# Identity matmuls ahead of the slot layer's transposes, sums and projections

## The chip, the cores and the metric

The kernel runs as one program on one core of a Trainium2 chip. The metric is the device time of one execution in microseconds (us). The kernel before takes 2276.86 us, the median of three runs (2275.09 to 2281.09 us).

The engines are named as in the profile: PE is the matrix engine, PEld its weight loads, DVE the vector engine, ACT the scalar engine, POOL the general engine, and SP the engine that issues most of the DMAs. Each engine works through its own instructions in order; between engines, instructions wait for semaphores.

## The reference

A residual network of eight sublayers works on `x` of 4 batches, 1024 tokens and 128 features, all in float32; after each sublayer comes a layer norm over the features of the sum of the input and the sublayer's output. The sublayers are a two-layer minGRU, the slot layer, a sparse attention, a two-expert feed-forward, a linear attention, a routed feed-forward with eight experts, a state-space scan and a second routed feed-forward. The change touches the slot layer and the step behind it:

```python
h = gelu(concat([x, slot_mean]) @ w1 + b1)                 # 64 hidden features
logits = (h @ w2 + b2) / (abs(tau) + 0.1)                  # 64 slots
alpha = softmax of the top 8 logits, scattered to the 64 slots
si = einsum('bts,btd->bsd', alpha, x) / (alpha.sum(1) + 1e-8)
S_new = GRU cell(si, slot_init)                            # gates r, z and n
q, k, v = S_new @ wq + bq, S_new @ wk + bk, S_new @ wv + bv
y = layernorm(S_new + softmax(q k^T * DQ**-0.5) v) * ln_g + ln_b
out = einsum('bts,bsd->btd', alpha, y @ wvp + bvp) @ wo + bo
x = layernorm(x + out)
```

The sparse attention that follows projects queries and keys of `x`, measures each query against 35 sampled keys (maximum less mean), and attends only for the 35 best queries of each head.

## The kernel before, in words

Tokens are held twice: `xN[b]` has 128 tokens on the partitions and eight chunks of 128 features, and `xT[b]` has the 128 features on the partitions and 1024 tokens. `to_features` makes the second from the first with PE transposes (the helper `tr`, L133, multiplies by the identity `self.ident`) into a PSUM bank called `pt`, four chunks to a bank, and an ACT copy (L143). All other matmuls go through the helper `mm` (L129), so the profile shows most of them under that one line and tells them apart by their tiles.

`front` runs the first sublayers. Generators for the batches are taken in turn by `weave`, which only sets the order in which instructions are written. The final order on each engine is set by a scheduler that plays the program on a timeline of its own, and that keeps to the data's order and to the PSUM banks. For the slot layer the eight banks are divided into the pools `u` (two banks, used by the update and by the first choice of queries), `p0` (three banks, batches 0 and 2) and `p1` (three banks, batches 1 and 3). These pool names exist in `self.psq` in this stage only; the minGRU ahead of it and the attention behind it use other names. In the linear attention (`l2_attn`) the order on PE is written out by hand.

The slot layer's steps, with the tile names under which the profile shows them:

- `l0_route`, once for each batch: `ph` (two halves of 512 tokens) and a Gelu on ACT into `hT`, which has two buffers; the logits `pl` (eight matmuls of 64 columns) and their copy `lg` on ACT (L302); on DVE the eight largest of each token (L306, L307) and the masked exponentials `ex`; the weights `al` on POOL (L321); eight transposes of `al` and an ACT copy into `alT`; the slot sums `psi`, eight matmuls that accumulate; on DVE the quotient `si` (L342), one transpose of it, and the ACT copy `siT`.
- `l0_update`, once, for all batches together: gates `pg` and `pn`, with DVE and ACT between them; `sn`, the new slots; the projections `pq` (twice, queries and keys) and `pv`; the scores `psc`; a softmax on DVE and ACT into `sat`; its transposes `pat`; the sum `py` (for each batch one matmul by the identity and one by the attention); a norm on DVE; the transposes `pyt`; the projections `psv` and `pso`, and the DVE copy into `svo`.
- `l0_read`, for batches 0 and 1 and then, beside the first choice of queries, for 2 and 3: for each half of the tokens `po` (four matmuls), a DVE sum into `slot_r` (L479), `norm_parts` on DVE and ACT (which writes `xN` at L176), and `to_features`. Each half is stored to DRAM (`xd`) by SP.
- `l1_measure` follows for each batch: `px` (sums of the sampled tokens by a one-hot matrix, 35 columns), `pk`, `pq` (512 columns), `pm` (280 columns) and a DVE maximum of it into `mall` (L569). `l1_choose` transposes `mall`, copies it to `mT` (L583), takes five rounds of top-8 on DVE (L588 to L591) and casts the indices (L595 to L600); SP takes them through DRAM, and POOL gathers the chosen rows (`xgs`, L645).

Of the kernel before, what the change touches and what calls it, by code (L numbers as in the profile page):

```python
# [20 lines left out]
P = 128  # L21
# [39 lines left out]
class Net:  # L61
# [66 lines left out]
    def mm(self, out, lhsT, rhs, start=True, stop=True):  # L128
        return self.nc.tensor.matmul(out=out, lhsT=lhsT, rhs=rhs, start=start, stop=stop)  # L129

    def tr(self, out, in_):
        n = in_.shape[0]
        self.nc.tensor.transpose(out, in_, self.ident[0:n, 0:n])  # L133

    def to_features(self, src, b, c0, g, ps=None):

        for c1 in range(0, g, 4):
            n = min(4, g - c1)
            pt = ps([P, n, P], "pt")
            for c in range(n):  # L140
                self.tr(pt[:, c, :], src[:, c1 + c, :])
            o = (c0 + c1) * P
            self.nc.scalar.copy(  # L143
                self.xT[b][:, o : o + n * P], pt.rearrange("p a b -> p (a b)")
            )
# [141 lines left out]
    def l0_route(self, b, ps, W, wp):  # L287

        nc, alT = self.nc, W["alT"][b]
        hT = wp.tile([DH + 1, T], F32, name="hT")  # L290
        nc.gpsimd.memset(hT[DH : DH + 1, :], 1.0)
        for h in range(2):
            s = slice(h * 512, h * 512 + 512)
            ph = ps([DH, 512], "ph")
            self.mm(ph, W["w1"][:, 0, :], self.xT[b][:, s])
            nc.scalar.activation(hT[0:DH, s], ph, AF.Gelu, bias=W["hb"])
        yield
        pl = ps([P, NC, NS], "pl")
        for k in range(NC):
            self.mm(pl[:, k, :], hT[:, k * P : (k + 1) * P], W["w2"])  # L300
        lg = wp.tile([P, NC, NS], F32, name="lg")
        nc.scalar.copy(lg, pl)  # L302
        top = wp.tile([P, NC, 8], F32, name="top")
        rep = wp.tile([P, NC, NS], F32, name="rep")
        for k in range(NC):
            nc.vector.max(top[:, k, :], lg[:, k, :])  # L306
            nc.vector.match_replace(rep[:, k, :], top[:, k, :], lg[:, k, :], NEG)  # L307

        ex = wp.tile([P, NC, NS], F32, name="ex")
        nc.vector.tensor_tensor(  # L310
            ex, pl, top[:, :, 0:1].to_broadcast([P, NC, NS]), ALU.subtract
        )
        nc.vector.tensor_tensor(rep, rep, pl, ALU.not_equal)
        nc.scalar.activation(ex, ex, AF.Exp, scale=W["rt"])
        yield
        nc.vector.tensor_mul(ex, ex, rep)
        es = wp.tile([P, NC], F32, name="es")
        nc.vector.reduce_sum(es, ex, AX.X)
        nc.vector.reciprocal(es, es)
        al = wp.tile([P, NC, NS], F32, name="al")  # L320
        nc.gpsimd.tensor_mul(al, ex, es[:, :, None].to_broadcast([P, NC, NS]))  # L321
        yield
        dn = wp.tile([NS, 2], F32, name="dn2")
        for h in range(2):
            pt = ps([NS, 4, P], "pt")
            for k in range(4):
                self.tr(pt[:, k, :], al[:, 4 * h + k, :])
            nc.scalar.activation(
                alT[0:NS, h * 512 : h * 512 + 512],
                pt.rearrange("p a b -> p (a b)"),  # L330
                AF.Copy,
                accum_out=dn[:, h : h + 1],
            )
        psi = ps([NS, D], "psi")
        for k in range(NC):
            self.mm(psi, al[:, k, :], self.xN[b][:, k, :], k == 0, k == NC - 1)
        yield
        rd = wp.tile([NS, 1], F32, name="rd")
        nc.vector.tensor_scalar(rd, dn[:, 0:1], dn[:, 1:2], 1e-8, ALU.add, ALU.add)
        nc.vector.reciprocal(rd, rd)  # L340
        si = wp.tile([NS, D], F32, name="si")
        nc.vector.tensor_scalar_mul(si, psi, rd)  # L342
        pt = ps([P, NS], "pt")
        self.tr(pt, si)
        nc.scalar.copy(W["siT"][:, b, :], pt)
        yield

    def l0_update(self, ps, W, pool):
# [20 lines left out]
            rz.append(g)  # L369
        yield  # L370
        pn = ps([P, 2, BS], "pn")
        self.mm(pn[:, 1], wg[:, 1, 2 * D :], s2)
        self.mm(pn[:, 0], wg[:, 0, 2 * D :], si)
        nn = wp.tile([P, BS], F32, name="nn")
# [13 lines left out]
        qk = []  # L388
        for w, nm in ((wq, "s_bq"), (wk, "s_bk")):
            pq = ps([DQ, BS], "pq")  # L390
            self.mm(pq, w, snf)
            t = wp.tile([DQ, N, NS], F32, name=f"t_{nm}")
            nc.vector.tensor_scalar_add(
                t.rearrange("p b s -> p (b s)"), pq, self.col(nm, DQ)
            )
            qk.append(t)
# [4 lines left out]
        nc.vector.tensor_add(v, pv, rows[:, 0:1, :].to_broadcast([NS, N, D]))  # L401
        yield
        psc = ps([NS, N, NS], "psc")
        for b in range(N):
            self.mm(psc[:, b, :], qk[0][:, b, :], qk[1][:, b, :])
        mx = wp.tile([NS, N], F32, name="smx")
# [8 lines left out]
        nc.vector.reciprocal(mx, mx)  # L415
        nc.vector.tensor_mul(at, at, mx[:, :, None].to_broadcast([NS, N, NS]))
        pat = ps([NS, N, NS], "pat")
        for b in range(N):
            self.tr(pat[:, b, :], at[:, b, :])
        att = wp.tile([NS, N, NS], F32, name="satT")  # L420
        nc.vector.tensor_copy(att, pat)
        yield
        py = ps([NS, N, D], "py")
        for b in range(N):
            self.mm(py[:, b, :], sn[:, b, :], self.ident, start=True, stop=False)
            self.mm(py[:, b, :], att[:, b, :], v[:, b, :], start=False, stop=True)
# [17 lines left out]
        nc.vector.tensor_add(y, y, rows[:, 2:3, :].to_broadcast([NS, N, D]))  # L444
        yield
        pyt = ps([P, N, NS], "pyt")
        for b in range(N):
            self.tr(pyt[:, b, :], y[:, b, :])
        yT = wp.tile([P, BS], F32, name="syT")
        nc.vector.tensor_copy(yT, pyt.rearrange("p b s -> p (b s)"))  # L450
        yield
        psv = ps([P, BS], "psv")
        self.mm(psv, wvp, yT)
        svT = wp.tile([P, N, NS], F32, name="svT")
        nc.vector.tensor_scalar_add(
# [2 lines left out]
        yield  # L458

        pso = ps([NS, N, D], "pso")  # L460
        for b in range(N):
            self.mm(pso[:, b, :], svT[:, b, :], wo)
        nc.vector.tensor_copy(W["svo"][0:NS], pso)
# [1747 lines left out]
```

## Time and profile before

| What | Value |
|---|---|
| Median of three runs | 2276.86 us (2275.09, 2276.86, 2281.09) |
| The profiled execution: its time, its span | 2279.28 us, 2277.5 us |
| Busy of the span: PE, PEld, DVE, ACT, POOL | 1977.3, 1385.7, 1348.0, 1198.7, 1024.1 us |
| Matmul passes on PE | 17788 |
| Mean clock of PE | 0.935 of full speed |
| Route (first `ph` to last `psi`) | 79.84 to 118.9 us |
| Update (first `pg` with `siT` to `svo`) | 120.24 to 148.5 us |
| Read and measure, batches 0 and 1 | 148.58 to 192.05 us |
| Read and measure, batches 2 and 3 | 191.49 to 242.8 us |

The profile comes from one execution, and its times are positions in its span. An engine's idle time ahead of an instruction is put down to what ended it ("<-"). In a timeline, a row stands for instructions of one form in succession: start, length from the first start to the last end, engine, line, operation, output and inputs, shape, count. The clock of PE is the share that the throttle granted, from 0.5 to 1.00 in this trace.

### The profile page before, as it was taken

How to read it: one execution, taken by the hardware profiler on the slowest of the kernel's cores; microseconds unless marked ns; L12 is line 12 of the kernel's file. 1: busy time of each engine (PE TensorE's matmuls, PEld its weight loads, DVE VectorE, ACT ScalarE, POOL GpSimd, SP SyncE). 2: the span in 40 equal slices, each digit the busy share in tenths (PEclk: the TensorE clock that was granted, in tenths of full speed). 3: DMA queues.
4: the chain of work that ended last, by engine and by line, in shares of the span. 5: the costliest groups of instructions: out<-in, count | busy, mean ns of one | idle time of the engine just before them, and what ended most of it. 6: DMA issues, size and time to landing. Idle time of an engine off the chain costs nothing.

```text
span 2277.5 us, 46329 instructions
## 1 busy us (share of the span) xinstructions
PE 1977.3 (87%) x17788; PEld 1385.7 (61%) x17788; DVE 1348.0 (59%) x3668; ACT 1198.7 (53%) x2610; POOL 1024.1 (45%) x812
## 2 busy tenths in 40 slices
PE   6667979979999999999979876679899999998998
PEld 3455655544477777787867664346565656565666
DVE  7647743433355555655565556696877688777521
ACT  6523433332244444444555455577768786767443
POOL 5100320000123235234243318998889989879400
PEclk9667989979999999999999987799999999999999
DMA  3000110005000010031222047456776677776421
GB/s 107 0 19 19 34 35 10 10 25 159 1 3 3 3 36 21 16 89 44 80 77 83 25 131 231 129 175 207 209 212 174 183 188 190 194 187 177 110 61 51
DMA packets 138555, 211.09 MB, mean 93 GB/s; under 512 B 18596, under 2 KB 75933, under 8 KB 137950
## 3 DMA queue, kind: packets, MB, share of 16 engines
q1 hardware_dynamic: 126190, 173.87, 25.4%
q0 software_dynamic: 12144, 34.26, 7.2%
q8 instruction: 140, 2.29, 0.4%
q14 instruction: 81, 0.66, 0.1%
HBM read 160.29 MB, written 23.16 MB: 81 GB/s over the span
## 4 chain that ended last, share of the span: by engine, by line
PE 43%; DVE 13%; ACT 11%; issue 3%; POOL 1%; DMA 1%; SPq 0%; ACTq 0%; DVEq 0%; POOLq 0%
PE py L129 8%; PE ph L129 7%; PE po L1127 5%; PE pqk L129 5%; PE pa_m L129 4%; DVE db L1855 4%; PE kp_mo L129 2%; PE pys L129 2%; PE pv L129 2%; PE pr L1197 2%; ACT da L1854 2%; ACT hh L1981 1%; PE pt L133 1%; PE kp_mo L133 1%; ACT xN L176 1%
## 5 line engine op out<-in xcount | busy, mean ns | idle before, releaser
L1060 POOL TENSOR_TENSOR qt<-r_q,sb_c_turn 128x256 f32<-128x256 f32 (+1 forms) x256 | 164.4, 663 | 451.5 <-ACT r_q L1052 445.9
L1866 POOL TENSOR_TENSOR hc<-db,cn 128x1024 f32<-128x1024 f32 x128 | 317.9, 2522 | 55.7 <-PE pys L129 28.2
L129 PEld LDWEIGHTS py<-wh,hh 128*128 128x128 f32 x2048 | 252.1, 193 | 81.6 <-issue 46.2
L1850 POOL TENSOR_TENSOR db<-ud,bn 128x1024 f32<-128x1024 f32 x112 | 290.7, 2679 | 12.4 <-issue 9.9
L129 PE MATMUL py<-wh,hh 128*128 128x128 f32 x2048 | 259.8, 278 | 14.2 <-ACT hh L1981 7.5
L129 PE MATMUL ph<-xT,wh 128*128 128x512 f32 x512 | 253.1, 610 | 21.3 <-DVE h_acc L1997 6.2
L1981 ACT ACTIVATE hh<-ph,sb_cols 128x512 f32<-128x512 f32 x256 | 170.6, 681 | 119.9 <-PE ph L129 93.2
L1118 DVE TENSOR_TENSOR a<-pa_m,sb_c_near 128x256 f32<-128x256 f32 x256 | 96.5, 419 | 205.0 <-PE pa_m L129 205.0
L1075 ACT ACTIVATE kN<-kp_mo,sb_c_trig 128x128 f32<-128x128 f32 x448 | 130.2, 372 | 131.5 <-PE kp_mo L133 121.6
L1854 ACT ACTIVATE da<-dl,aneg 128x512 f32<-128x512 f32 x224 | 153.4, 689 | 76.1 <-DVE db L1855 75.0
L129 PE MATMUL pys<-hc,sb_c_ident 128*128 128x512 f32 x324 | 159.6, 623 | 21.6 <-POOL hc L1866 19.6
L1855 DVE TENSOR_TENSOR_SCAN db<-da,carry,db 128x512 f32<-128x512 f32 x128 | 157.0, 1265 | 13.3 <-ACT da L1854 9.4
L1855 DVE TENSOR_TENSOR_SCAN db<-da,db 128x512 f32<-128x512 f32 x128 | 149.2, 1204 | 10.4 <-POOL db L1850 6.0
L129 PEld LDWEIGHTS ph<-xT,wh 128*128 128x128 f32 x512 | 88.4, 193 | 101.7 <-issue 52.4
L1997 DVE SCALAR_TENSOR_TENSOR h_acc<-py,gt,h_acc 128x128 f32<-128x128 f32 x256 | 71.9, 342 | 129.5 <-PE py L129 129.5
L129 PE MATMUL pqk<-xT,wE 128*128 128x256 f32 x512 | 138.3, 394 | 8.2 <-ACT coT L1194 4.2
L129 PEld LDWEIGHTS pys<-hc,sb_c_ident 128*128 128x128 f32 x324 | 61.1, 200 | 85.6 <-issue 59.0
L731 POOL DMA_INDIRECT orows<-o,ix x20 | 18.9, 946 | 187.5 <-DVE o L729 160.9
L129 PEld LDWEIGHTS pqk<-xT,wE 128*128 128x128 f32 x512 | 89.6, 195 | 22.2 <-DVE cv L1037 8.1
L1194 ACT COPY coT<-pt 128x512 f32<-128x512 f32 x64 | 37.6, 587 | 117.1 <-PE pt L133 117.1
L133 PE MATMUL pt<-sb_c_ident,xN 128*128 128x128 f32 x224 | 52.7, 342 | 48.7 <-ACT xN L176 29.0
L129 PE MATMUL po<-ht,wD 128*128 128x512 f32 x192 | 93.7, 595 | 0.0
(453 smaller groups left out, 4328.5 us busy)
## 6 DMA issues: line engine op xcount, KB each, us to landing
wx<-in_wF SPq DMA_DIRECT2D x92, 384.0 KB, 3.5
bn<-rows SPq DMA_DIRECT2D x128, 256.0 KB, 4.7
cn<-rows SPq DMA_DIRECT2D x128, 256.0 KB, 4.2
wh<-in_wH SPq DMA_DIRECT2D x64, 512.0 KB, 3.8
hc<-hc POOLq DMA_DIRECT2D x47, 512.0 KB, 6.6
xrows<-zero SPq DMA_DIRECT2D x4, 1472.0 KB, 13.1
xg<-xrows SPq DMA_DIRECT2D x20, 256.0 KB, 3.2
yrows<-ys SPq DMA_DIRECT2D x20, 256.0 KB, 3.2
```

The lines of the kernel that those rows point to most:

```text
L129: return self.nc.tensor.matmul(out=out, lhsT=lhsT, rhs=rhs, start=start, stop=stop)
L133: self.nc.tensor.transpose(out, in_, self.ident[0:n, 0:n])
L1060: nc.gpsimd.tensor_mul(u["qt"][:, m, a:], u["q"][:, a:], c2["turn"][:, m, o + a : o + 2 * P])
L1075: self.nc.scalar.activation(u["kN"][:, c, m, :], pk[:, c, :], AF.Copy, scale=trig[:, k, m : m + 1])
L1118: nc.vector.tensor_mul(u["a"][:, i, :, :], pa[i], self.c2["near"][:, None, :].to_broadcast([P, 2, P]),)
L1127: self.nc.tensor.matmul(out=u["po"][self.HALF[j], i, c, :], lhsT=lhsT, rhs=rhs, start=key not in u["begun"], stop=True, skip_group_check=True,
L1850: nc.gpsimd.tensor_mul(db, ud, bc[0])
L1854: nc.scalar.activation(da, dl[:, ec, :], AF.Exp, scale=aneg[:, j : j + 1])
L1855: nc.vector.tensor_tensor_scan(db[:, ec, :], da, db[:, ec, :], carry[:, ec, n : n + 1] if h else 0.0, ALU.mult, ALU.add,)
L1866: nc.gpsimd.tensor_mul(hc, db, bc[1])
L1981: nc.scalar.activation(ht, ph, AF.Relu, bias=self.col("h_b1", i=e * NK + k))
L1997: nc.vector.scalar_tensor_tensor(acc[:, c, :], py[:, c, :], gt[:, c, e : e + 1], acc[:, c, :], ALU.mult, ALU.add,)
```

## The change

A helper `warm` writes `n` matmuls (eight unless said otherwise) of the identity by the identity into a tile that the code is about to fill. It does so only where the pool `p0` exists, that is in this stage. It is called ahead of the transposes in `to_features`, of the logits `pl` and the slot sums `psi` in the route, and of `pn`, `pq` (4 each), `psc`, `pat`, `py`, `pyt`, `psv` and `pso` in the update. The real matmuls start their banks anew, so the results of the helper are overwritten.

```diff
+    def warm(self, out, n=8):
+
+        if "p0" in self.psq:
+            p, o = out.shape[0], out[:, 0] if len(out.shape) == 3 else out
+            for k in range(n):
+                self.mm(o, self.ident[:, 0:p], self.ident[:, 0 : o.shape[1]])
...
             pt = ps([P, n, P], "pt")
+            self.warm(pt)
             for c in range(n):
                 self.tr(pt[:, c, :], src[:, c1 + c, :])
...
         pl = ps([P, NC, NS], "pl")
+        self.warm(pl)
...
         psi = ps([NS, D], "psi")
+        self.warm(psi)
...
         pn = ps([P, 2, BS], "pn")
+        self.warm(pn[:, 0, 0:P], 8)
...
             pq = ps([DQ, BS], "pq")
+            self.warm(pq[:, 0:P], 4)
...
         psc = ps([NS, N, NS], "psc")
+        self.warm(psc, 8)
...
         pat = ps([NS, N, NS], "pat")
+        self.warm(pat, 8)
...
         py = ps([NS, N, D], "py")
+        self.warm(py, 8)
...
         pyt = ps([P, N, NS], "pyt")
+        self.warm(pyt, 8)
...
         psv = ps([P, BS], "psv")
+        self.warm(psv[:, 0:P], 8)
...
         pso = ps([NS, N, D], "pso")
+        self.warm(pso, 8)
```

In the changed program's order on PE, the helper's matmuls stand as follows. Those of `pl` are directly ahead of each batch's logits. Those of `psi` are behind the eight transposes of `al` of the same batch, directly ahead of the slot sums. In the update they are directly ahead of their real matmuls, but for `py` (its helper matmuls and its first real one stand ahead of the transposes `pat`) and `psv` (ahead of the transposes `pyt`). In the read of batches 0 and 1, 16 stand between the first and the second halves' `po` and 16 more ahead of and among the first transposes; in that of batches 2 and 3, 5 stand between the two first `po`, 11 behind the second, 12 behind the second halves' `po`, and 4 among the transposes. The helper adds 192 matmuls in all.

## The prediction

> **What bounds the kernel now.** I read the page's slices first, then windows of 25 and 2 us over the slot layer, the waits in it, and the timelines of PE, DVE, ACT and POOL from 80 to 330 us. The chain that ended last is followed back only to 613.99 us, so it says nothing of the slot layer (75 to 250 us); from there on it is one unbroken chain, so what the slot layer gains or loses should reach the end about one to one.
>
> ```profile
> PE   6667979979999999999979876679899999998998
> PEclk9667989979999999999999987799999999999999
> ```
> One digit is 57 us. The clock is below full in the first slices, where PE is also the least busy.
>
> ```profile
> 100.00:125.00 25.00, 16.50 (x108) 13.34 (x108) 17.61 (x75) 8.47 (x25) 4.17 (x4) 0.82 0.00 1
> 125.00:150.00 25.00, 14.78 (x60) 9.18 (x61) 10.44 (x30) 2.00 (x3) 0.00 (x0) 0.59 0.00 0
> 150.00:175.00 25.00, 21.19 (x87) 17.76 (x86) 9.95 (x50) 11.43 (x29) 0.00 (x0) 0.52 0.15 43
> 175.00:200.00 25.00, 18.77 (x98) 11.07 (x96) 19.05 (x59) 5.85 (x11) 0.00 (x0) 0.95 0.00 1
> 200.00:225.00 25.00, 18.12 (x73) 15.48 (x74) 23.59 (x60) 10.81 (x26) 4.67 (x2) 0.50 0.14 42
> ```
> Columns: length, then busy time of PE, PEld, DVE, ACT and POOL, then the clock. From 125 to 175 us PE runs at half clock and is the busiest engine; from 200 us DVE is, with 23.6 of 25 us. A faster PE is thus worth much in the first stretch and little in the second.
>
> In the 2 us windows the clock steps at 95.4 (down), 109.0 (up), 126.1 (down), 129.5 (up), 132.9 (down), 173.9 (up), 197.8 (down), 225.1 (up): all apart by multiples of 3.41 us. It falls after a stretch that was mostly idle (122.64 to 125.59) or held only the 64-column logits (pl, 91.9 to 95.4). It does not rise from 163.6 to 170.4, when PE runs transposes and 35-column px without a break, and rises once pq of 512 columns fills a stretch.
>
> ```profile
> PE pt L133 <- ACT xN L176: 16.9, 4, 6.6
> PE pt L133 <- POOL al L321: 9.8, 2, 9.7
> ```
> Of PE's waits, these two are the long ones.
>
> ```profile
> 86.89 2.00 PE L129 MATMUL pl<-sb_w_slot,hT 65*128 65x64 f32 x16
> 109.81 1.06 PE L133 MATMUL pt<-sb_c_ident,al 128*64 128x128 f32 x8
> 110.81 1.96 PE L129 MATMUL psi<-xN,al 128*64 128x128 f32 x16
> 125.59 1.49 PE L129 MATMUL pq<-sn,sb_w_slota 128*32 128x256 f32 x4 [2.95 <-DVE sn L385]
> 127.01 1.97 PE L129 MATMUL pv<-sb_w_slota,sn 128*64 128x128 f32 x8
> 132.43 0.38 PE L133 MATMUL pat<-sb_c_ident,sat 64*64 64x64 f32 x4 [2.60 <-DVE sat L416]
> 142.86 0.66 PE L133 MATMUL pyt<-sb_c_ident,sy 64*128 64x64 f32 x4 [5.16 <-DVE sy L444]
> 169.69 3.76 PE L129 MATMUL pq<-xT,sb_w_sp 128*128 128x512 f32 x4
> ```
> A matmul of f32 is two passes here (8 psi matmuls are x16). A pass of 128 columns takes 0.122 us at full clock (psi) and 0.246 at half (pv); so one warm of eight 128-column matmuls takes 1.96 or 3.9 us, and one of 64 columns into 128 rows 1.9 us (pl).
>
> **The change, part by part.** It adds 192 matmuls (384 passes) on PE in banks that the real work then overwrites, removes none, and issues no DMA. Each warm waits for its bank alone, and everything later on PE waits behind it. Where it stands in PE's order decides. L2's own order on PE is unchanged; later orders differ only by swaps of a few places (L3 among them), for which I take 0 and 3 us either way.
>
> Route, warms of pl (four times 16 passes). Before, PE ran from 79.84 to 95.4 without a wait, so nothing hides them. The first logits end at about 91.7 instead of 88.85; ACT does two Gelus first (they wait for hT, which the logits free), and lg goes from 90.14 to 93.05. DVE starts 2.9 us later. The new DVE order finishes batch 0 before going on, so al of batch 0 comes at 106.7 instead of 105.1 on PE.
>
> Route, warms of psi. In the new order they stand behind the transposes of al, which wait for POOL: the 9.7 us wait is not filled. Each batch now takes PE 1.0 (pt) + 1.96 (warm) + 1.96 (psi) = 4.9 us, where batches came every 3.1 us (109.81, 112.92, 116.01). From 106.7 the first takes 1.9 + 3.9 + 2.0 us while the clock is still half, the others 4.9 each: the last psi ends at 129.2 instead of 118.9, and pg, 1.3 us later, starts at 130.5 instead of 120.24: +10.2 us. If the clock stays full before al, +8.5; if the longer pl stretch loses it at 95.4, its last 64 passes run at 0.21 us (px x10 in 2.19 us at half clock, also small columns) instead of 0.12, al of the later batches comes late, and it is +13. I take +11, nearer to the upper end since the trace does lose the clock in pl.
>
> Update (times relative to pg). The warm of pn has no wait to hide in: pn came 0.1 us after pg. It delays nn by 1.3 us (DVE's gates end only at 122.66). The warm of pq (2 x 4) lies in the 2.95 us wait for sn. pq, pv and psc drop from 4.24 to 2.4 us at full clock, less 0.85 for psc's warm: now +0.5. pat's and py's warms (0.85 + 1.96) and the first py (0.25) stand ahead of pat and exceed the 2.60 us wait, since py's bank is free only after DVE's sat: +1.2. py's eight pairs go from 5.0 to 2.3 us: -1.35. pyt's and psv's warms (3.9) lie in the 5.16 us wait; pyt and psv get 0.9 us shorter: -2.2. pso's warm (1.96) has a 0.58 us wait: +1.4; pso is 1.0 shorter: -1.8; the first po 0.95 shorter, so DVE's slot_r starts 2.85 us earlier than it would.
>
> Read of batches 0 and 1. 32 warm matmuls, 7.8 us at full clock. The first 16 run while DVE and ACT normalise; po of the second halves, which stood behind the first transposes, now stand before them. Second halves reach ACT's xN 0.8 to 1.5 us earlier; px, pt, pk and pq run in 11 instead of 16 us. The first pm comes at 170.4 instead of 177.29: -6.9 from pg on, update included. The other end: the stretch of pt and px loses the clock as it failed to raise it in the trace, pk comes 2.5 us later and pq runs at half clock again: -1.9. I take -4.
>
> The Trainium skill ("TensorE: Matmul & The Clock Gate", Part 4) states that transposes do not count as PE being busy. The row of 163.6 to 170.4 agrees, that of 105.1 to 109.0, where transposes filled 1.8 us of the stretch and the clock rose, does not; by the page this term would be near its end of -1.9, by the second row near -6.9.
>
> Read of batches 2 and 3. DVE runs mall from 180.64 and is idle 10.4 us in all until 246.0 (0.64, 1.23, 3.57, 2.13, 2.55, 0.28), which is the most that can be won. Five warms delay the second po and mT by 1.2 us; the rest fit in the 6.63 and 6.48 us waits. The index cast (L600) stands later on DVE, so SP's index DMAs and POOL's ten gathers (12.4 us from 226.97) start some 2.6 us later; they land just in time. Followed through the new DVE order, top-k of batches 2 and 3 starts 5.8 us earlier from the first pm on; with PE at half clock again, 2. I take -4. From there the DVE sequence to the next index cast is as long as before (28.5 against 28.1 us).
>
> Sum: +11 - 4 - 4 = +3 us on the profiled execution of 2279.28 us (span 2277.5 and 1.8 around it). It lies 2.4 us above the median of the runs, 2276.86 (2275.09 to 2281.09); against the median: **2280 us**.
>
> The same page (Part 1) states that the clock falls only after an idle window of about 3.4 us. The row of 122.64 to 125.59 fell after 2.95 us, so the row is used; by the page the 2.95 and 2.60 us waits would need no warming, and the update would be a loss of some 5 us where I have a gain of 2.85.
>
> **The rivals.**
> Slower: the clock is lost in pl and in both stretches of pt and px. Ends +13, -1.9, -2: +9, with the reordered tail up to +12: 2286 to 2289 us. For it: both kinds of stretch lost or failed to raise the clock before. Against: psi and pt kept it full from 109 to 122. It decides once psi starts at half clock and PE, behind, pushes pg past 132.
> Faster: the clock holds throughout (+8.5, -6.9) and DVE closes all its idle time (-10.4): -8.8, 2268 us. For it: half of PE's 36 us from 125 to 175 are there to win. Against: DVE needs mall, top-k and norms one after the other, and ACT's xN paces the transposes.
> The warms do not raise the clock at all: at 3.9 us each they would cost about 13 us in the route, 16 in the update, 11 and 5 in the reads: +45, 2322 us. Against: psi, of the same shape, raised it at 109.0.
>
> **How the numbers follow.** Forecast +3: 0.44. Clock lost in between: 0.32. No rise at all: 0.07. Clock held and DVE packed: 0.17. A measurement of this kernel can tell about 0.3%, 6.8 us: faster 0.17, same 0.44, slower 0.39. Range: from the faster rival, 2268, to a little beyond the middle slower one, 2291; outside are the last rival and the far ends.
>
> **What would show it.** Right: psi of the four batches about 4.9 us apart, pg near 131, clock 1.00 in most of 125 to 165, first mall (L569 before) 5 to 9 us late, top-k of batches 2 and 3 within 3 to 5 us of its old place. Wrong: psi's warms ahead of al; half clock from 130 to 160; a last DVE step of the layer that stays late by more than 10; or a stage behind 300 us that is no longer the same length.

## The result, and the profile after

The changed kernel takes 2286.13 us (median of 19 runs), the kernel before, run beside it 19 times, 2280.22 us. The ratio is 1.0024, 95% interval 1.0014 to 1.0034: +5.5 us of 2280, from 3.2 to 7.8. That lies within the 0.3% named as "no change", 6 us above the forecast and inside the range, but the interval leaves out 1: the change makes the kernel a little slower. Of the 6 us, 3.4 are the kernel before, whose median rose from 2276.86 us (three runs) to 2280.22 (19). The profiled execution took 2286.13 us, with a span of 2284.4 us.

The page's slices of PE and of its clock, in the changed kernel:

```profile
PE   6889979879999999999979876679889999998998
PEclk9698979979999999999999988799999999999999
```
The second to fourth digits (57 to 228 us) hold the slot layer. PE is busier there (8, 8, 9 where it was 6, 6, 7), and the clock has 6, 9, 8 where it had 6, 6, 7. The change does what it says, and yet it loses time.

The windows over that layer (length; busy time of PE, PEld, DVE, ACT, POOL; then the clock, the DMA share and GB/s):

```profile
100.00:125.00 25.00, 24.14 (x150) 22.66 (x150) 15.87 (x80) 6.89 (x17) 4.13 (x4) 0.71 0.00 1
125.00:150.00 25.00, 22.53 (x186) 18.02 (x184) 8.48 (x22) 5.04 (x13) 0.00 (x0) 1.00 0.01 2
150.00:175.00 25.00, 22.41 (x195) 21.30 (x194) 14.24 (x63) 7.86 (x22) 0.00 (x0) 1.00 0.08 22
175.00:200.00 25.00, 25.00 (x140) 15.95 (x139) 15.41 (x48) 8.49 (x17) 0.00 (x0) 1.00 0.08 22
200.00:225.00 25.00, 21.08 (x125) 17.24 (x124) 24.96 (x66) 11.48 (x29) 4.66 (x2) 0.77 0.15 43
```
From 125 to 200 us the clock is 1.00, where it was 0.59, 0.52 and 0.95. From 100 to 125 us it is 0.71, lower than the 0.82 of before, although PE is now busy for 24.1 of 25 us. It was lost in the logits, as this timeline of PE shows (start, length, operation, output and inputs, shape, passes):

```profile
91.25 1.95 PE L129 MATMUL pl<-sb_c_ident 128*128 128x64 f32 x16
93.03 2.59 PE L129 MATMUL pl<-sb_w_slot,hT 65*128 65x64 f32 x16
95.42 3.62 PE L129 MATMUL pl<-sb_c_ident 128*128 128x64 f32 x16
98.83 3.62 PE L129 MATMUL pl<-sb_w_slot,hT 65*128 65x64 f32 x16
102.24 3.62 PE L129 MATMUL pl<-sb_c_ident 128*128 128x64 f32 x16
105.66 3.62 PE L129 MATMUL pl<-sb_w_slot,hT 65*128 65x64 f32 x16
109.07 1.92 PE L140 MATMUL pt<-sb_c_ident,al 128*64 128x128 f32 x8
110.91 3.68 PE L129 MATMUL psi<-sb_c_ident 128*64 128x128 f32 x16
114.38 2.04 PE L129 MATMUL psi<-xN,al 128*64 128x128 f32 x16
```
The clock around it, in windows:

```profile
91.93:95.34 3.41, 3.41 (x28) 3.41 (x28) 2.07 (x20) 1.31 (x3) 0.58 (x1) 0.83 0.01 2
112.39:115.80 3.41, 3.41 (x23) 3.41 (x22) 3.41 (x22) 1.23 (x3) 0.00 (x0) 0.67 0.02 5
```
A mean of 0.83 over 3.41 us is full clock until 94.2 and half from there; 0.67 is half until 114.7. In between, two warms and two batches of logits run at half clock, 3.41 us from start to start for 16 passes of 64 columns. The transposes of al start at 109.07 instead of 105.08, and not because al is late: POOL has it ready at 108.30 (107.26 and 1.04 us), and PE comes from its last logits. The first psi starts at 114.38. The last batch of the route, and the first gates behind it:

```profile
126.62 1.06 PE L140 MATMUL pt<-sb_c_ident,al 128*64 128x128 f32 x8
127.62 1.96 PE L129 MATMUL psi<-sb_c_ident 128*64 128x128 f32 x16
129.41 1.91 PE L129 MATMUL psi<-xN,al 128*64 128x128 f32 x16
132.86 1.13 PE L129 MATMUL pg<-siT,sb_w_gru 128*128 128x256 f32 x4 [0.30 <-ACT siT L355]
```
This batch costs PE 1.0 + 1.8 + 1.8 us back to back, and pg starts 12.6 us later than before (120.24). Four of PE's waits from 75 to 250 us, the whole slot layer (time in all, times, longest):

```profile
PE pt L140 <- ACT xN L184: 2.5, 2, 2.0
PE pyt L140 <- DVE sy L459: 1.3, 1, 1.3
PE pq L129 <- DVE sn L396: 0.8, 1, 0.8
PE pt L140 <- POOL al L330: 0.6, 1, 0.6
```
The wait for xN was 16.9 us and is 2.5, that for al was 9.8 and is 0.6, that for sy was 5.2 and is 1.3: the first and the last are filled with warms, the one for al with logits at half clock. What is left of the wait for xN (0.5 and 2.0 us) lies in the read of batches 2 and 3. A filled wait is no gained time; what counts is when the next engine gets its data. The first maximum of the measure, the first top-8 of batches 2 and 3 on DVE, and a matmul at the head of the linear attention on PE, first in the kernel before and then in the changed one:

```profile
178.06 0.45 DVE L569 TENSOR_REDUCE mall<-pm 128x8 f32<-128x280 f32 x1 [3.38 <-PE pm L129]
245.98 1.22 DVE L588 MAX8 t<-mT 32x8 f32<-32x1024 f32 x1 [0.28 <-ACT mT L583]
614.04 0.44 PE L133 MATMUL kp_mo<-sb_c_ident,r_k 128*128 128x128 f32 x2 [1.06 <-ACT r_k L1052]
...
183.00 0.45 DVE L587 TENSOR_REDUCE mall<-pm 128x8 f32<-128x280 f32 x1 [3.25 <-PE pm L129]
249.40 1.22 DVE L606 MAX8 t<-mT 32x8 f32<-32x1024 f32 x1 [0.24 <-ACT mT L601]
617.38 0.44 PE L140 MATMUL kp_mo<-sb_c_ident,r_k 128*128 128x128 f32 x2 [1.06 <-ACT r_k L1070]
```
So the delay is 12.6 us at pg, 4.9 at the first maximum, 3.4 at the top-8, and 3.3 at 615 us. Behind that the two executions drift by up to 2.5 us both ways (+5.4 at 909 us, +3.5 at 1211, +5.7 at 1920).

### The profile page after: what moved, and what is told of

It is laid out like the page before. It is cut to its first block, busy times and chain, and to the rows that moved or that the text cites. A ratio compares the mean times of both kernels' runs of the same rounds, so it can differ in the third digit from the quotient of the medians.

```text
span 2284.4 us, 47094 instructions
## 1 busy us (share of the span) xinstructions
PE 2011.5 (88%) x18172; PEld 1420.2 (62%) x18172; DVE 1348.6 (59%) x3668; ACT 1197.9 (52%) x2610; POOL 1024.0 (45%) x812
## 4 chain that ended last, share of the span: by engine, by line
PE 44%; DVE 12%; ACT 11%; issue 3%; DMA 1%; POOL 1%; SPq 0%; ACTq 0%; DVEq 0%; POOLq 0%
PE py L129 8%; PE ph L129 7%; PE po L1145 5%; PE pa_m L129 4%; PE pqk L129 4%; DVE db L1873 4%; PE kp_mo L129 3%; PE pys L129 2%; PE pr L1215 2%; PE pv L129 2%; ACT da L1872 2%; ACT hh L1999 2%; PE pt L140 1%; PE kp_mo L140 1%; ACT xN L184 1%
## 5 line engine op out<-in xcount | busy, mean ns | idle before, releaser
L129 PE MATMUL py<-wh,hh 128*128 128x128 f32 x2048 | 259.0, 277 | 13.7 <-ACT hh L1999 7.0
L1999 ACT ACTIVATE hh<-ph,sb_cols 128x512 f32<-128x512 f32 x256 | 170.4, 680 | 130.9 <-PE ph L129 104.4
L1145 PE MATMUL po<-cv,a 128*64 128x65 f32 x2048 | 89.2, 230 | 0.0
## 6 DMA issues: line engine op xcount, KB each, us to landing
xrows<-zero SPq DMA_DIRECT2D x4, 1472.0 KB, 12.6
```

Of the source, the lines that this page charges most:

```text
L1145: self.nc.tensor.matmul(out=u["po"][self.HALF[j], i, c, :], lhsT=lhsT, rhs=rhs, start=key not in u["begun"], stop=True, skip_group_check=True,
L1999: nc.scalar.activation(ht, ph, AF.Relu, bias=self.col("h_b1", i=e * NK + k))
```

## The experiments

Theory: the route's warms cost 10 to 13 us, since nothing covers them, and the warms of the update and the reads gain by the clock, some 9 us together. Rivals: the later gain is only other engines catching up with a late route; or the gain comes from the new order of instructions; or the late stages, which the scheduler has written in another order, make the difference.

The first eight runs were made on a chip where the kernel before takes 2280.54 and 2281.24 us, the last four (reads_8col, pl_wide, cover, all_pt7) on another, where it takes 2324.33 us; for these only ratios are compared with the rest, and positions only up to 250 us. A ratio is turned into us by the time of the kernel before that stands beside it.

### no_route

```diff
-        self.warm(pl)
-        self.warm(psi)
```


> The changed kernel without the warms of pl and psi. My theory: the route's warms cost 12.6 us at pg (120.24 to 132.86) and all else is gain: from pg to the first top-k of batches 2 and 3 the changed kernel is 9.2 us shorter (7.7 up to the first pm, 1.5 after it). So pg is back at 120.2 to 120.4, the first pm at about 169.6 (177.29 before), and the end 6 to 9 us below the kernel before: 2271 to 2274, ratio 0.996 to 0.9975. Rival: those 9.2 us were only won because other engines caught up while the route was late, and are no gain of the clock: then the first pm stays within 2 us of 177.3 and the time within 2 us of before, 2279 to 2282.

Measured: ratio 0.9959 (0.9944 to 0.9974), -9.3 us. pg at 119.89, first pm at 169.24. The windows of this kernel:

```profile
125.00:150.00 25.00, 20.84 (x179) 17.18 (x179) 12.23 (x35) 2.50 (x4) 0.00 (x0) 1.00 0.00 1
150.00:175.00 25.00, 25.00 (x171) 19.70 (x169) 11.74 (x56) 15.11 (x34) 0.00 (x0) 1.00 0.15 43
```
The clock is full in the update and the read without any help in the route. The gain stays when the route is not late, so it is no catching up. The two deleted lines turn the change into a faster kernel.

### route_only

```diff
         pl = ps([P, NC, NS], "pl")
+        self.warm(pl)
...
         psi = ps([NS, D], "psi")
+        self.warm(psi)
```


> The kernel before with the warms of pl and psi alone. My theory: pg at about 132.9, nothing after it is shorter, so the delay reaches the end whole: +10 to +13 us, 2290 to 2293, ratio 1.0045 to 1.0055. Rival: the later stages swallow a part of any delay (waits for ACT's xN, POOL's gathers, DVE's idle 10.4 us), whatever the clock: +3 to +6 us, 2283 to 2286, the same as the whole change.

Measured: ratio 1.0046 (1.0032 to 1.006), +10.5 us. pg at 133.82, first pm at 191.36. In this kernel every engine's order behind the route is that of the kernel before, so the delay is priced alone: it is 14.1 us at the first pm of the profile (1.3 of them from ahead of the route), and 10.5 (7.3 to 13.7) at the end by the ratio, so the later stages swallow little of it, if any.

### update_only and update_pn6

update_only has the eight warms of the update and no other; update_pn6 differs from it in one line:

```diff
-        self.warm(pn[:, 0, 0:P], 8)
+        self.warm(pn[:, 0, 0:P], 6)
```


> The kernel before with the eight warms of the update alone. My theory: pg at 120.2, the clock stays full from there to about 147 instead of falling at 126.1, slot_r starts 1.4 to 2.9 us earlier than at 150.69, and with half clock again in the reads the end moves by -1 to -3 us: 2277 to 2279. Rival: the clock is lost all the same (the warms are 35 per cent of the stretch) and each warm costs its 2 to 3.9 us where no wait covers it: slot_r 4 to 8 us late, 2284 to 2288.

> update_only with six warm matmuls for pn in place of eight. By the front this is the same kernel (0.5 us of PE less), but from the reads on every engine's order is that of the kernel before, where update_only's last 40 per cent were written in another order (nearly 1000 of PE's instructions elsewhere). My theory: the loss of 17 us of update_only is the late order's alone, and the update's warms are worth -1 to -3 us: 2277.5 to 2279.5, ratio 0.9987 to 0.9996. Rival: the warms cost it, for instance by a clock that is lost later: 2290 or more.

Measured: update_only 1.0073 (1.0058 to 1.0087), +16.6 us; update_pn6 0.9996 (0.9984 to 1.0009), -0.9 us. Both have full clock from 125 to 147 us, and both reach the first pm a little early (175.54 and 175.44, before 177.29). So update_only was missed by 18 us, and nothing in the front up to there explains it. What differs is the order of the last 40 per cent of the program, on all engines, a thousand microseconds behind the edit. PE's waits from 1500 to 2290 us, first in update_pn6:

```profile
PE py L129 <- ACT hh L1996: 8.3, 11, 2.7
...
PE ph L129 <- ACT hh L1996: 5.0, 6, 1.7
PE psk L129 <- ACT hh L1996: 4.2, 4, 1.5
```
and in update_only:

```profile
PE ph L129 <- ACT hh L1996: 16.9, 10, 3.5
PE py L129 <- ACT hh L1996: 14.1, 13, 4.3
```
For ACT's hh, the hidden features of the last routed feed-forward, PE waits 31.0 us there and 32.3 with two small rows (psk 0.7, pt 0.6); in update_pn6 it is 17.7 with one small row (0.2). The profiles agree with these 14.6 us: update_only is 4.6 us behind update_pn6 at the head of the linear attention (615.81 against 611.22), ahead of most of the new order, and 19.3 at the end (spans of 2290.8 and 2271.5), so 14.7 us are lost behind it. The loss by the runs is 0.77% of 2280, 17.6 us (13 to 22). That two warm matmuls and the order make it is shown; that the waits for hh are its path is argued from this agreement. The warms of the update by themselves are worth between -3.6 and +2.1 us.

### reads_only

```diff
             pt = ps([P, n, P], "pt")
+            self.warm(pt)
```


> The kernel before with the warms of the features' transposes (pt) alone. My theory: the clock is still half when the first 32 warm matmuls start (about 152 us), they take 7.5 us for 64 passes at 0.24, two thirds of it in the wait for ACT's xN, and raise the clock one or two steps of 3.4 us later; px, pt, pk and pq then run at full clock: first pm 3 to 5 us earlier than 177.29, end -2 to -5 us, 2275 to 2278. Rival: the transposes and the 35-column px lose the clock again, and the warms only delay them: first pm 0 to 3 us late, 2280 to 2284.

Measured: ratio 0.9956 (0.9939 to 0.9972), -10.0 us, twice what was expected; the medians, 2273.3 and 2280.54 us, differ by 7.2. First pm at 173.56, 3.7 us early as expected. The second read, with which I had not reckoned, gives as much again: the transposes of its maxima start at 235.55, before at 244.17, and the clock is 1.00 from 215 us on (0.68 from 210 to 215), where it was 0.50 up to 225. By 280 us the kernel is 8.1 us ahead. One line of the change gives all that the best version gives.

### one_psc

reads_only and the changed kernel also have another late order, though a smaller one. This run has almost nothing but that order:

```diff
         psc = ps([NS, N, NS], "psc")
+        self.warm(psc, 1)
```


> The kernel before with a single warm matmul, of 64 columns, ahead of the scores psc. It adds 0.25 us to PE, but the scheduler answers it with another order of the last tenth of the program (37 of PE's instructions, 54 of DVE's, 26 of ACT's, 42 of SP's stand elsewhere), which is the very order that reads_only has there. My theory: that order of the tail costs 1 to 3 us by itself (the changed kernel goes from +5.7 at 2000 us to +6.9 at the end, reads_only from -2.8 to -1.7): 2281 to 2283, ratio 1.0004 to 1.0013, up to 250 us nothing. Rival: the late order costs nothing, and what the stages gain or lose there is how the clock's steps happen to fall: 2280 within 1 us.

Measured: ratio 0.9993 (0.9981 to 1.0005). The theory fell: this late order costs nothing that can be told (-4.3 to +1.1 us), and my reading of the last part of the traces (up to 2 us there) was the drift of single executions. Since psi_first, below, has this late order too (but for a few places near 700 us), the gains of reads_only and psi_first are not the late order's.

### all_pt10

```diff
-            self.warm(pt)
+            self.warm(pt, 10)
```


> The whole change with ten warm matmuls ahead of the transposes in place of eight: 16 matmuls more, 2 us at full clock after what hides in waits, and from the third tenth on the order of the kernel before on every engine but for a few places. My theory: the front is +4 to +6 (the change was +3.3 at 615 us), the later stages keep that: 2284 to 2286, ratio 1.0017 to 1.0026. Rival: the change's +5.9 us are all front, its late order costs nothing, and two more warms per bank add to it: 2288 to 2290.

Measured: ratio 1.0022 (1.001 to 1.0034), +5.0 us, with the late order of the kernel before. The whole change, with 16 warms more, costs the same with the old late order as with the new one: the loss is made in the front. Its first pm is at 185.37, 3.2 us behind the changed kernel's. Of that, 1.4 us are there at the first slot_r (163.31 after 161.94), ahead of the added warms, because the clock falls to half from 156.4 to 159.8 us; the rest comes in the read. By the top-8 the two are level (249.08 and 249.40).

### psi_first

```diff
         dn = wp.tile([NS, 2], F32, name="dn2")
+        psi = ps([NS, D], "psi")
+        self.warm(psi)
         for h in range(2):
             pt = ps([NS, 4, P], "pt")
...
-        psi = ps([NS, D], "psi")
-        self.warm(psi)
...
-        self.warm(pl)
```


> The whole change without the warms of pl, and with those of psi ahead of the transposes of al instead of behind them. On PE's order the warms of batches 0 and 1 now stand ahead of the first transposes, in the 9.7 us wait for POOL's al. My theory: those two cost nothing and keep the clock full, those of batches 2 and 3 cost 1 to 2 us each, pg at 121 to 124 (132.86 in the changed kernel, 119.89 in no_route), and the rest is as in no_route: 2273 to 2276, ratio 0.997 to 0.9985. Rival: the route pays for each warm wherever it stands: pg at 127 or later, 2279 to 2281.

Measured: ratio 0.9969 (0.9956 to 0.9982), -7.1 us; pg at 122.59. Against no_route's 119.89 the four warms cost 2.7 us instead of the 8 that they take on PE, because those of batches 0 and 1 lie in the wait for al. They still gain nothing: the clock was full at pg without them.

### reads_8col

reads_only with the helper's matmuls 8 columns wide, twelve to a bank:

```diff
-                self.mm(o, self.ident[:, 0:p], self.ident[:, 0 : o.shape[1]])
+                self.mm(o[:, 0:8], self.ident[:, 0:p], self.ident[:, 0:8])
...
-            self.warm(pt)
+            self.warm(pt, 12)
```


> reads_only with warm matmuls of 8 columns, twelve to a bank in place of eight of 128. The order is that of reads_only but for places in the second tenth, and from the third tenth on it is the same. My theory: reads_only gains by the clock, and a pass must stream columns to hold it (the 64-column logits lost it, the 35-column px did not raise it): the clock stays at 0.50 through the first read, first pm at 177 to 180 (173.56 in reads_only), the end 0 to +4 us from before: ratio 1.000 to 1.002. Rival 1: the clock counts that PE is busy, whatever the columns: it rises as in reads_only, ratio 0.995 to 0.9975. Rival 2: the gain is the new order's (second po ahead of the first transposes), not the clock's: ratio 0.995 to 0.9975 though the clock is half.

Measured: ratio 1.0111 (1.0089 to 1.0134), +26 us of 2324; pg at 120.5, first pm at 194.14. Two of its rows on PE and three of its windows:

```profile
152.54 7.26 PE L129 MATMUL pt<-sb_c_ident 128*128 128x8 f32 x34
...
167.58 7.26 PE L129 MATMUL pt<-sb_c_ident 128*128 128x8 f32 x34
```
```profile
155.00:160.00 5.00, 5.00 (x25) 5.00 (x26) 0.34 (x2) 3.14 (x9) 0.00 (x0) 0.50 0.37 105
160.00:165.00 5.00, 5.00 (x26) 5.00 (x25) 0.00 (x0) 1.17 (x2) 0.00 (x0) 0.50 0.01 3
...
185.00:190.00 5.00, 5.00 (x14) 2.93 (x13) 0.86 (x3) 0.88 (x2) 0.00 (x0) 0.50 0.01 3
```
reads_only in the same stretch:

```profile
152.89 4.82 PE L129 MATMUL pt<-sb_c_ident 128*128 128x128 f32 x32
```
```profile
155.00:160.00 5.00, 5.00 (x47) 5.00 (x46) 1.38 (x8) 3.96 (x10) 0.00 (x0) 0.98 0.31 89
```
PE is busy for every microsecond from 150 to 190 us, and the clock stays at 0.50 until pq of 512 columns fills a stretch (0.91 from 190 to 195). A pass of 8 columns takes 0.21 us there (7.12 us from this row's start to the next row's, for 34), nearly as long as one of 128 at half clock. So it is not being busy that raises the clock, and rival 1 falls. Rival 2 is not tested by this kernel: its po of the second halves stands behind the first transposes (164.17), as in the kernel before, while in reads_only it stands ahead of and among them. What speaks against rival 2 is the time of equal work: from the first px to the first pm PE takes 9.8 us in reads_only (163.79 to 173.56) and 15.5 in the kernel before (161.82 to 177.29), for the same passes of px, pk and pq, without a wait in either. The size was missed (0 to +4 us expected): I had not counted that 24 passes at 0.21 us, 5.0 us to a bank, lie open when the clock does not rise.

### pl_wide

```diff
-        self.warm(pl)
+        self.warm(pl[:, 0:2, :].rearrange("p a b -> p (a b)"))
```


> The whole change, with the warms of pl over 128 columns (two chunks of the bank at a time) in place of 64, as many and as long. By its end it says nothing of the warms: its late order is that of update_only. Theory: the clock is lost at 95 us because half of the columns of a pass are missing; with 128 in half of the passes it holds, the last pl ends near 102 instead of 109.1 us and pg starts at 127 to 129 (132.86). Rival: the columns do not matter, or half of the passes are not enough: the clock falls in the same place and pg starts at 132 to 134.

Measured once: 2334.37 us. Its timeline of PE:

```profile
95.69 2.00 PE L129 MATMUL pl<-sb_c_ident 128*128 128x128 f32 x16
97.53 1.90 PE L129 MATMUL pl<-sb_w_slot,hT 65*128 65x64 f32 x16
99.26 2.00 PE L129 MATMUL pl<-sb_c_ident 128*128 128x128 f32 x16
101.10 1.90 PE L129 MATMUL pl<-sb_w_slot,hT 65*128 65x64 f32 x16
106.85 1.92 PE L140 MATMUL pt<-sb_c_ident,al 128*64 128x128 f32 x8 [3.85 <-POOL al L330]
```
With 128 columns in every other group the clock holds through the logits: the last pl ends at 103.0, not 109.3. It is lost after that, near 105.5, in the wait for al, and pg starts at 129.58, 3.3 us before the changed kernel's. The warms of pl were thus too narrow for what they were there for. But even with the clock full in the logits they cost 9.7 us together with psi's (129.58 against 119.89 in no_route).

### cover

Only the warms that lie in waits:

```diff
-        self.warm(pl)
-        self.warm(psi)
-        self.warm(pn[:, 0, 0:P], 8)
-        self.warm(psc, 8)
-        self.warm(pso, 8)
```


> The version that the runs so far point to: the warms that lie in waits (pt, pq, pat, py, pyt, psv), without those of the route (pl, psi) and without those that delay their own step (pn, psc, pso). My theory: reads_only's -7.2 us with the update's -1 to -2 on top, as far as the late order (one that no run here had) allows: 2270 to 2274, ratio 0.9955 to 0.997. Rival: the late order decides, as in update_only: 2280 or more.

Measured: ratio 0.9969 (0.9955 to 0.9983), at the upper end of what was expected. From pg to the first slot_r it takes 26.5 us (28.6 in update_pn6, 30.5 before), so the three warms without cover do cost 2.1 us; by the end this is not seen, and its late order is one that only this run has. no_route, reads_only, psi_first and cover beat both kernels; their intervals overlap, so which of them is best stays open.

### all_pt7

```diff
-            self.warm(pt)
+            self.warm(pt, 7)
```


> The whole change with seven warm matmuls ahead of the transposes in place of eight, 16 matmuls less in all. Up to the third tenth its order is nearly that of the changed kernel; the last 40 per cent are in the order of update_only. Theory: that late order costs 15 to 18 us wherever the front ends (update_only 1.0073 against update_pn6 0.9996): the time is 2300 to 2304, ratio 1.0085 to 1.0105, and the front is within 2 us of the changed kernel's. Rival: update_only lost its time by where its own clock steps fell, not by the order: 2285 to 2288, ratio 1.002 to 1.003.

Measured: ratio 1.0047 (1.0031 to 1.0063), between theory and rival. PE's waits from 1500 us on are those of update_only:

```profile
PE ph L129 <- ACT hh L1999: 16.5, 10, 3.5
PE py L129 <- ACT hh L1999: 13.4, 12, 4.3
```
But against the changed kernel's 1.0024 the time is only 0.23% longer here (0.04 to 0.42), though PE's waits for hh in these two rows alone are 29.9 us and in the changed kernel 12.9. So a longer wait for hh need not reach the end whole. Whether the other chip hides a part of it was not tried. So the price of that late order is open: 17.6 us (13 to 22) in one pair of kernels, about 5 (1 to 10) in this one.

## Why the prediction was right or wrong

The runs' front, in us of each profile:

| Kernel | pg | first pm | pg to pm | ratio at the end |
|---|---|---|---|---|
| before | 120.24 | 177.29 | 57.1 | 1 |
| changed | 132.86 | 182.22 | 49.4 | 1.0024 |
| route_only | 133.82 | 191.36 | 57.5 | 1.0046 |
| update_pn6 | 120.97 | 175.44 | 54.5 | 0.9996 |
| reads_only | 121.00 | 173.56 | 52.6 | 0.9956 |
| no_route | 119.89 | 169.24 | 49.4 | 0.9959 |

- **Route, +11 taken: +12.6 by the trace, +10.5 alone in route_only.** The mechanism and its upper end (+13, "if the longer pl stretch loses it at 95.4") were right. The mis-sized term is the clock in pl: I took a point between the ends, and the clock fell, at 94.2 us. With that, PE began the transposes of al at 109.07 and not at 106.7, behind its own logits, with al ready at 108.3; the prediction had them wait for POOL. DVE's first top-8 was 2.5 us late (93.27 after 90.75; 2.9 forecast). The lower end, +8.5, is not what its pieces add up to: from 106.7, four batches of 4.9 us and 1.3 more give 127.6, +7.4. Only the faster rival rests on it.
- **Update, -2.85 at slot_r: -1.4.** The pieces, from pg: pn +1.8 (1.3), pat +1.9 (1.2), sy's copy +0.1 (-1.35), slot_r -1.4. Each of these terms came out 0.5 to 1.5 us less good than worked out. It is small either way, as update_pn6 says.
- **Read of batches 0 and 1 with the update, -4 taken: -7.7.** This is beyond the favourable end, -6.9. The clock held through transposes and 35-column px, from 172.4 to 176.4 us. The Trainium skill ("TensorE: Matmul & The Clock Gate", Part 4) would have put it near -1.9; the row that speaks against it, weighed in the prediction, was the better guide here. In these traces the clock changes only at steps of 3.41 us, and one whole step, 172.7 to 176.1, held nothing but px and transposes; in no_route the step from 159.4 to 162.8 did too, but for its first 0.1 us, and the clock stayed. At half clock the same mix had not raised it (163.6 to 170.4 in the kernel before). Transposes alone were not tried.
- **Read of batches 2 and 3, -4 taken: -1.5** (4.9 us late at the first maximum, 3.4 at the top-8). The unfavourable end, -2, came true: the clock fell at 213.6 us, when PE waited for ACT's xN and ran 35-column px between, and pq ran at half clock (3.76 us).
- **Sum: +3 forecast, +3.4 at the top-8 and +3.3 at 615 us.** The number is right by luck, because the misses cancel: +1.6, -3.7 and +2.5. route_only, reads_only and update_pn6 sum to -0.4 us alone, 6 us less than the whole change; their intervals (about 3 us each way) leave that open.
- **Later stages, "0 and 3 us either way".** For this change it held (one_psc, all_pt10). As a rule it was wrong: update_only lost 16.6 us through a late order that two warm matmuls fewer undo. My range (to 2291) would not have held such a case, and no rival named it.
- **Rivals.** The warms raise the clock, so that rival is out. Of the slower rival the first part came true (pl) and the second only in batches 2 and 3; its sign, psi at half clock and pg past 132, was seen (110.91 and 132.86), its +9 was not. The faster one failed at both its conditions.

## What to carry to other kernels

A matmul that keeps the clock up is free only where PE would have waited; look for where it stands in PE's order, since behind the awaited transposes it fills nothing and delays the sums. Before the waits are filled one by one, try the one place with the longest wait (here ACT's xN): one line gave -10 us, eleven places +5.5. Where a scheduler writes the order, a change may cost more by what it does to an order a thousand microseconds behind than by itself (update_only), so hold the order fixed, by a count that leaves it alone, before a small effect is believed.

## What the runs showed of the hardware

- It is not PE being busy that brings up the clock, and the width of the passes counts. PE without a gap, on 8-column passes for 7.1 us at a time, transposes, po and 35-column px, left it at 0.50 from 150 to 186 us in reads_8col; 64-column logits with 64-column warms lost it at 94.2 us; and with 128-column warms of the same number and length they held it (pl_wide). The Trainium skill ("TensorE: Matmul & The Clock Gate", Part 1) says that whatever is issued in the first 3.4 us of work runs slow and everything after it fast. The runs do not fit a count of time alone: in reads_only the 128-column warms raised it within 2.3 us (from 152.9 to 155.2), in reads_8col the 8-column ones did not.
- Columns are not all of it. In reads_8col po, 128 columns of 65 rows, filled 2.9 of the 3.4 us from 163.6 to 167.0, and the clock stayed at 0.50; in reads_only 2.3 us of warms, 128 columns of 128 rows, behind 1.1 us of po raised it at 155.2. That the rows count as well fits both, but no run tried it by itself.
- At half clock a pass of 8, of 64 and of 128 columns takes 0.209, 0.213 and 0.217 us from start to start (34 passes from 152.54 to 159.66 in reads_8col; 16 of pl from 95.42 to 98.83 and 16 of psi from 110.91 to 114.38 in the changed kernel): a narrow pass is hardly cheaper than a wide one.
- Less than a whole idle step was enough to lose the clock: a wait of 2.5 us in pl_wide, behind 0.9 us of 64-column logits (PE ends at 103.0, the clock falls near 105.5), and in all_pt10 two waits of 1.30 and 0.52 us in the step from 153.0 to 156.4. The changed kernel kept it through the same two waits, which lie otherwise to the steps there.
